# Rows of a graph layer scattered in groups of four, each group tied to TensorE's progress in the next block

## The chip, the core and the metric

The kernel runs on one core of one Trainium2 chip. The metric is device time in microseconds (us) of one execution; the time of a kernel is the median of several. Times inside an execution are read from a hardware trace of one profiled execution.

## The reference, cut to what matters

There are 6,250 nodes with 64 features, 206,250 directed edges (each drawn edge in both directions and one loop per node, sorted by destination before the call) with 64 features each. Per edge a first layer with 128 hidden values is computed; the hidden values are summed per target node and counted. What follows is small and per node.

```python
msg = concat([x[col], edge_attr], axis=1)          # per edge, 128 values
h = relu(msg @ W1a.T + b1a)                        # per edge, 128 hidden values
h = h @ W1b.T + b1b
sums = segment_sum(h, row, num_segments=n_nodes)   # summed per node
agg = sums / maximum(counts, 1)[:, None]
z = relu(concat([x, agg]) @ W2a.T + b2a) @ W2b.T + b2b
x = layernorm(x + concat([z, x]) @ Wr.T + br)
```

The kernel sums `relu(...)` per node, and applies `W1b` after the sum.

## The kernel before, in words

**Blocks.** The edges are cut into 124 blocks (`NGR`) of 13 tiles (`BLK`) of 128 edges. Edges of a block belong to scattered nodes, so they are sorted on the chip: the kernel computes the hidden values of a block's edges, counts with one-hot matmuls which slot of a table in DRAM each edge gets (slots are grouped by bins of 128 nodes), and GpSimd (POOL in the profile) scatters the rows there with indirect DMAs. A row is 130 numbers: 128 hidden values, a one for the count, and the node's place in its bin. Some blocks later the SyncE queue reads whole bins back in tiles of 128 rows (`read`, L1454), VectorE makes one-hot matrices of them (`nodes_of`, L1483) and TensorE sums a bin with one matmul per tile (`summed`, L1502); VectorE adds the result to the node's total (`collect`, L1562).

**Two kinds of block.** In blocks 4 to 103 ("joined" here) a part of the tiles goes another way: groups of 3 tiles (`JOIN`) are sorted inside the block by matmuls with one-hot `marks` (`join`, L1264), copied by ScalarE to `rj` (L1269), taken through the first layer (`join_rows`, L1277, with the ReLU at L1280), and scattered four rows at a time as a "quad" (L1363). `joined(k)` is 2 (3 in every second block from 9 to 25), so such a block has 2 quads and 7 single rows (`direct(k)`; 3 quads and 4 rows with three groups). The other blocks, "direct" here, have 13 single rows. A "row" below is one indirect DMA of L1392: one tile of 128 edges, 128 x 130 numbers. There are 985 rows and 209 quads in all. A row's number `j` is its tile's number in the block: 6 to 12 with two groups, 9 to 12 with three, 0 to 12 in direct blocks.

**One pass of the main loop (block k) on TensorE,** in this order: the counts of block k+1 (L1091 to L1095); all but the last part of the block's first layer (`hidden`, L1352, its ReLU L1355 writes `orow`); the ranks of the groups of block k+1 (`join_ranks`, L1118 to L1130), which need `of_quads` (L1105) from VectorE, which needs the counts; the first half of a group of sums (`sum_first`); the last part of `hidden`; `join` for groups 0 and 1; `join_rows` for group 0, then 1 (a third group follows in the same way); the second half of the sums (`sum_rest`), and in the direct blocks further whole groups of sums (`sum_next`). Sums are dealt out by `RATES`: about 13 tiles per joined block, 9 with three groups, and up to 50 in direct blocks.

**What sets the order.** TensorE, ScalarE, VectorE and SyncE work in the written order (`manual_schedule`). GpSimd's order is the framework's: it sorts the scatters by when they can go by its own plan, so that rows with nothing to wait for move ahead of others. `scatter(k)` issues the quads and rows of a block. Four buffers of rows (`ROWS`) let several blocks stand open. Each DMA goes to one of eight semaphores in turn (DMASW0 to DMASW7 in listings) and waits for the DMA that had it before.

**The pace.** For blocks 9 to 117 (`PACED`, L474) some rows of block k also wait for a matmul of block k+1, by the table `pace`: with two groups row 6 for column 9 of `hidden` (the end of its first part), row 8 for column 12 (the end of its last part), row 10 for `join_rows` 0, row 12 for `join_rows` 1; in direct blocks row 0 for column 9, row 2 for the first half of the sums, row 7 for column 12, row 11 for the rest of the sums. The rows between have no such wait. Blocks 118 to 123 have none at all.

## Time and profile before

| | |
|---|---|
| median of 3 runs | 2108.51 us (2105.86 to 2118.02) |
| profiled execution | 2113.43 us, span in the trace 2111.6 us |
| TensorE | busy 1648.5 us, 78% of the span, 10901 matmuls |
| VectorE | busy 1376.4 us, 65% |
| GpSimd | busy 1153.6 us, 55% |
| ScalarE | busy 1105.0 us, 52% |
| mean DMA rate | 188 GB/s |

A page of the profile gives busy times per engine, the span in 40 slices, the chain of work that ended last, and the costliest groups of instructions (line, engine, operation, output and input, count, busy time, mean, and the idle time just ahead of them with what ended most of it). A table of windows gives the busy time of each engine in a stretch of the trace, with TensorE's granted clock as a share of full speed (PEclk), the mean busy share of the DMA engines and GB/s. A timeline lists instructions with start, length and, in brackets, the idle time of that engine before them and what ended it; "remote" and "issue" mean that no instruction on the core was found that ended it just then.

### The profile page before, as it was taken

To read this page: it belongs to the slowest core of one execution; us is meant where nothing else is said; L and a number is where in the kernel's file an instruction comes from. 1 tells how busy PE (TensorE), PEld (TensorE's weight loads), DVE (VectorE), ACT (ScalarE), POOL (GpSimd) and SP (SyncE) were. 2 spreads that over 40 slices of the span, in tenths; PEclk is the share of its full clock that TensorE was granted. 3 is DMA by queue.
4 is the path that set the end of the run, shared out by engine and by line. 5 is a ranking of instruction groups with operands and counts; after the bars stand their busy time and mean duration, and the time that the engine had idled before them with its cause. 6 is when DMAs were issued, how large, how long until landed. Compare 5 with 4: busy or idle time off the path is not lost.

```text
span 2111.6 us, 33441 instructions
## 1 busy us (share of the span) xinstructions
PE 1648.5 (78%) x10901; PEld 1455.0 (69%) x10901; DVE 1376.4 (65%) x3210; ACT 1105.0 (52%) x2246; POOL 1153.6 (55%) x1268
## 2 busy tenths in 40 slices
PE   5577877768887888788778887877867778677787
PEld 4466766657776777677667776776767667566676
DVE  5377777656667777677776777776755555454377
ACT  2257777666666566566666666656622223222007
POOL 6464655565555566566665665655655545544400
PEclk7578988889999899999998999989978878777899
DMA  6556667665656567566556555555668667565472
GB/s 163 162 171 220 234 224 243 214 211 176 209 183 204 169 201 211 169 195 188 181 174 182 175 173 163 186 157 170 168 201 277 200 190 208 170 183 172 147 216 66
DMA packets 243142, 396.32 MB, mean 188 GB/s; under 512 B 43621, under 2 KB 177895, under 8 KB 242703
## 3 DMA queue, kind: packets, MB, share of 16 engines
q1 hardware_dynamic: 162109, 225.24, 37.7%
q0 software_dynamic: 48240, 121.28, 16.4%
q10 hardware_dynamic: 32610, 47.58, 6.5%
q8 instruction: 89, 1.46, 0.3%
q14 instruction: 94, 0.77, 0.1%
HBM read 218.49 MB, written 175.44 MB: 187 GB/s over the span
## 4 chain that ended last, share of the span: by engine, by line
PE 57%; issue 11%; DVE 10%; ACT 10%; another core or an unknown queue 8%; DMA 3%; POOL 1%; SPq 0%; ACTq 0%; DVEq 0%; POOLq 0%
PE h_ps L1502 22%; PE h_ps L1264 10%; PE h_ps L1352 9%; PE h_ps L1277 7%; DVE oh L1483 2%; DVE marks L1232 2%; ACT rhs L1317 2%; ACT rj L1269 1%; ACT orow L1355 1%; DMA rows<-orow,rowidx 1%; DMA rt<-rows 1%; ACT orow L1280 1%; ACT marks L1237 1%; PE cnt_ps L1091 1%
## 5 line engine op out<-in xcount | busy, mean ns | idle before, releaser
L1392 POOL DMA_INDIRECT rows<-orow,rowidx x985 | 947.2, 962 | 769.4 <-issue 207.4
L1502 PE MATMUL h_ps<-rt,oh 128*128 128x129 f32 x4056 | 602.3, 303 | 126.4 <-issue 105.4
L1502 PEld LDWEIGHTS h_ps<-rt,oh 128*128 128x128 f32 x4056 | 554.3, 215 | 151.9 <-issue 135.7
L1355 ACT ACTIVATE orow<-h_ps 128x384 f32<-128x384 f32 (+1 forms) x287 | 153.3, 537 | 657.5 <-PE h_ps L1352 360.7
L1277 PE MATMUL h_ps<-mv,rj 128*128 128x130 f32 x1672 | 256.1, 305 | 136.3 <-ACT rj L1269 73.5
L1264 PE MATMUL h_ps<-marks,side 128*128 128x512 f32 x1254 | 343.7, 423 | 23.8 <-ACT xr_now L1652 10.6
L1277 PEld LDWEIGHTS h_ps<-mv,rj 128*128 128x128 f32 x1672 | 232.6, 210 | 174.4 <-ACT rj L1269 89.1
L1562 DVE TENSOR_TENSOR part<-part,h_ps 128x387 f32<-128x387 f32 (+2 forms) x249 | 122.6, 493 | 312.5 <-remote 147.7
L1483 DVE TENSOR_TENSOR oh<-ramp,rt 128x768 f32<-128x768 bf16 (+3 forms) x440 | 321.3, 765 | 7.2 <-DMA rt<-rows 7.0
L1352 PE MATMUL h_ps<-mv,rhs 124*128 124x128 f32 x1970 | 297.3, 298 | 16.8 <-issue 9.2
L1264 PEld LDWEIGHTS h_ps<-marks,side 128*128 128x128 f32 x1254 | 245.1, 204 | 79.5 <-issue 11.6
L1352 PEld LDWEIGHTS h_ps<-mv,rhs 124*128 124x128 f32 x1970 | 267.1, 209 | 20.4 <-issue 10.6
L1232 DVE TENSOR_TENSOR marks<-quad_ramp,ramp 128x1024 fp32r<-128x1024 f32 x209 | 250.9, 1204 | 0.0
L1363 POOL DMA_INDIRECT quads<-orow,qidx x209 | 200.4, 959 | 88.8 <-ACT orow L1280 39.1
L1280 ACT ACTIVATE orow<-h_ps 128x260 f32<-128x260 f32 x418 | 142.6, 388 | 90.8 <-PE h_ps L1277 28.0
L1105 DVE TENSOR_SCALAR of_quads<-cnt_ps 128x98 bf16<-128x98 f32 x100 | 26.6, 266 | 247.0 <-remote 84.2
L1269 ACT COPY rj<-h_ps 128x512 f32<-128x512 f32 x209 | 118.8, 588 | 120.8 <-PE h_ps L1264 67.6
L1238 ACT ACTIVATE marks<-marks,ones 128x512 fp32r<-128x512 f32 x209 | 151.0, 722 | 6.8
L1237 ACT ACTIVATE marks<-quad_ramp,z_act 128x512 fp32r<-128x512 f32 x209 | 149.5, 715 | 0.0
L1049 DVE TENSOR_TENSOR_SCAN had<-ramp,bins 128x400 bf16<-128x400 bf16 (+1 forms) x124 | 135.0, 1089 | 14.9 <-ACT bins L1070 1.2
L1315 ACT ACTIVATE rhs<-rhs,from_win 60x896 f32<-60x896 bf16 (+1 forms) x116 | 130.4, 1124 | 2.8
L1317 ACT ACTIVATE rhs<-rhs,ones 60x896 f32<-60x896 f32 (+1 forms) x116 | 130.2, 1123 | 2.9
(189 smaller groups left out, 1535.6 us busy)
## 6 DMA issues: line engine op xcount, KB each, us to landing
rt<-rows SPq DMA_DIRECT2D x138, 390.0 KB
rt<-quads SPq DMA_DIRECT2D x98, 390.0 KB
rhs<-in_edgeT SPq DMA_DIRECT2D x91, 224.0 KB
rt<-rows SPq DMA_DIRECT2D x103, 195.0 KB
enat<-in_edgeJ SPq DMA_DIRECT2D x91, 192.0 KB
rows<-orow,rowidx POOLq DMA_INDIRECT x985
rows<-padrow ACTq DMA_DIRECT2D x12, 1300.0 KB
quads<-padrow ACTq DMA_DIRECT2D x11, 1300.0 KB
```

Source lines behind the costliest of these rows:

```text
L1232: nc.vector.tensor_tensor(m[:, :n, :], all_q[:, None, :].to_broadcast([P, n, QUAD * P]), z[:, :n, None].to_broadcast([P, n, QUAD * P]), op ...
L1237: nc.scalar.activation(m[:, t, :], all_q, AF.Square, bias=z_acts[k][:, i * JOIN + t : i * JOIN + t + 1], scale=-1.0)
L1264: nc.tensor.matmul(ps, s[:, p, i * JOIN + t, :], m[:, t, :], start=t + p == 0, stop=t == JOIN - 1 and p == 1,)
L1277: done[k, f"join{i}"] = nc.tensor.matmul(ps[:, j, :], rj[:, (g0 + j) * P : (g0 + j + 1) * P], m, start=True, stop=True).ins.name
L1280: nc.scalar.activation(mrow[:, g0 : g0 + 2, :], ps, AF.Relu)
L1317: nc.scalar.activation(rhs[D:WIDE, :], rhs[D:WIDE, :], AF.Relu, bias=ones[D:WIDE, :1], scale=-1.0)
L1352: done[k, c] = nc.tensor.matmul(ps[:, j, :], rhs[:WIDE, of * P : (of + 1) * P], m[:WIDE, :H], start=True, stop=True).ins.name
L1355: nc.scalar.activation(orow_of(k, k0, n)[:, :, :H], ps[:, :n, :], AF.Relu)
L1363: s = nc.gpsimd.indirect_dma_start(out=qep.rows.rearrange("(q r) f -> q (r f)", r=QUAD), out_offset=bass.IndirectOffsetOnAxis(ap=qidx[:, q ...
L1392: s = nc.gpsimd.indirect_dma_start(out=ep_.rows, out_offset=bass.IndirectOffsetOnAxis(ap=rowidx[:, k % RING * BLK + j : k % RING * BLK + j ...
L1483: nc.vector.tensor_tensor(res[:, at_tile : at_tile + nb * n, :], ramp[:, None, :].to_broadcast([P, nb * n, P]), node[:, :, None].to_broadc ...
L1502: m = nc.tensor.matmul(of_bin(b), oh[:, at_tile, :], rt[:, j * n + t, : H + 1], start=t0 + t == st.lo[b], stop=t0 + t == st.hi[b] - 1,)
```

## The change

The table `pace` goes. Each piece of TensorE's work on a block is now written down as it is issued (`phase`): its size in matmul columns times passes, and its last matmul. `reached(k + 1, share)` gives the last matmul of block k+1 up to which at most that share of the block's written work is done; for a share of 0 that is the last one of block k itself. Every row of blocks 9 to 117 now waits for one of these. The share steps up after every fourth row, where the quads count as rows ahead: with two groups rows 6 and 7 have share 0, rows 8 to 11 have 4/9, row 12 has 8/9; with three groups row 9 has 0 and rows 10 to 12 have 4/7; in direct blocks rows 0 to 3 have 0, rows 4 to 7 have 4/13, rows 8 to 11 have 8/13 and row 12 has 12/13.

For a block with two groups and one group of 12 tiles of sums, the work is 20080 in all: 2048 `hidden`, 4128 first half of sums, 1536 `hidden` (7712 so far), two times 3072 `join`, two times 2080 `join_rows` (each written down in halves of 1040), 2064 rest of the sums. 4/9 of that is 8924, so rows 8 to 11 wait for the end of `hidden` in block k+1; 8/9 is 17849, so row 12 waits for the first half of the second `join_rows` (16976). A direct block has 6656 of `hidden` and, with 48 tiles, 24768 of sums; 4/13 of 31424 is 9669, so rows 4 to 7 wait for the first half of the first sums (9248).

```diff
@@ join
+            phase(k, 2 * JOIN * QUAD * P, name)
@@ join_rows
+                phase(k, 4 * W * 2, name)
@@
-        done = {}
+        phases = [[] for _ in range(NGR + 1)]
+        def phase(k, work, name):
+            phases[k].append(((phases[k][-1][0] if phases[k] else 0) + work, name))
+        def reached(k, share):
+            names = [name for at, name in phases[k] if at <= share * phases[k][-1][0]]
+            return names[-1] if names else phases[k - 1][-1][1]
@@ hidden
+                phase(k, 4 * H * n, name)
@@ scatter
-            pace = (
-                {9: BLK - 1, 10: "join0", 11: "join1", 12: "join2"} if j0 == 3 * JOIN
-                else {6: 9, 8: BLK - 1, 10: "join0", 12: "join1"} if j0 == 2 * JOIN
-                else {j0: 9, j0 + 2: "first", 7: BLK - 1, 9: "join0", 11: "rest"}
-            )
-                later = (min(k + 1, NGR - 1), pace.get(j))
-                if k in PACED and later in done:
+                later = reached(k + 1, (j - j0 + joined(k)) // 4 * 4 / (BLK - j0 + joined(k))) if k in PACED else None
+                if later:
-                        s.ins, done[later],
+                        s.ins, later,
@@ sum_first, and sum_rest in the same way
+            phase(k, *summed(g.st, g.reads, g.oh, lambda b: g.ps[:, b - g.b0, :], g.half))
```

The order of TensorE, ScalarE, VectorE and SyncE stays as it is; GpSimd's changes. Two places show it. In the rows below L1363 is a quad and L1392 a row of before, L1377 and L1401 the same of the change; `orow0` to `orow3` are the four buffers (block k uses buffer k mod 4), and the brackets hold what an instruction waits for.

GpSimd in the joined part before, from row 6 of block 61 (`orow1`), among rows of block 60 (`orow0`) and block 62 (`orow2`):

```order
L1392 DMA rows0_64<-orow1_142,rowidx_105 125440x130 [waits DMASW0_49,DVE_49,Activation_49]
L1392 DMA rows0_64<-orow1_142,rowidx_105 125440x130 [waits DMASW1_49]
L1392 DMA rows0_64<-orow0_141,rowidx_105 125440x130 [waits DMASW2_49,PE_49]
L1392 DMA rows0_64<-orow1_142,rowidx_105 125440x130 [waits DMASW3_49,Activation_49]
L1392 DMA rows0_64<-orow0_141,rowidx_105 125440x130 [waits DMASW4_49,PE_49]
L1363 DMA quads_67<-orow1_142,qidx_224 54976x520 [waits DMASW5_49,DVE_49,Activation_49]
L1392 DMA rows0_64<-orow0_141,rowidx_105 125440x130 [waits DMASW6_49,PE_49]
L1363 DMA quads_67<-orow1_142,qidx_224 54976x520 [waits DMASW7_49,Activation_49]
L1392 DMA rows0_64<-orow1_142,rowidx_105 125440x130 [waits DMASW0_49,PE_49]
L1392 DMA rows0_64<-orow2_143,rowidx_105 125440x130 [waits DMASW1_49,DVE_49,Activation_49]
L1392 DMA rows0_64<-orow2_143,rowidx_105 125440x130 [waits DMASW2_49]
L1392 DMA rows0_64<-orow1_142,rowidx_105 125440x130 [waits DMASW3_49,PE_49]
```

The same place after the change, from the first quad of block 61 to the second quad of block 62:

```order
L1377 DMA quads_67<-orow1_142,qidx_224 54976x520 [waits DMASW2_49,DVE_49,Activation_49]
L1377 DMA quads_67<-orow1_142,qidx_224 54976x520 [waits DMASW3_49,Activation_49]
L1401 DMA rows0_64<-orow0_141,rowidx_105 125440x130 [waits DMASW4_49,PE_49]
L1401 DMA rows0_64<-orow1_142,rowidx_105 125440x130 [waits DMASW5_49,PE_49]
L1401 DMA rows0_64<-orow1_142,rowidx_105 125440x130 [waits DMASW6_49]
L1401 DMA rows0_64<-orow1_142,rowidx_105 125440x130 [waits DMASW7_49,PE_49]
L1401 DMA rows0_64<-orow1_142,rowidx_105 125440x130 [waits DMASW0_49]
L1401 DMA rows0_64<-orow1_142,rowidx_105 125440x130 [waits DMASW1_49]
L1401 DMA rows0_64<-orow1_142,rowidx_105 125440x130 [waits DMASW2_49]
L1401 DMA rows0_64<-orow1_142,rowidx_105 125440x130 [waits DMASW3_49,PE_49]
L1377 DMA quads_67<-orow2_143,qidx_224 54976x520 [waits DMASW4_49,DVE_49,Activation_49]
L1377 DMA quads_67<-orow2_143,qidx_224 54976x520 [waits DMASW5_49,Activation_49]
```

Before, the rows of two blocks alternate, and rows of a block without a wait for TensorE go ahead of its quads; now a block's rows follow its quads, with a wait for TensorE at rows 6, 8 and 12.

GpSimd in the direct part before, from the first row to go of block 107 (`orow3`), among rows of block 106 (`orow2`):

```order
L1392 DMA rows0_64<-orow3_144,rowidx_105 125440x130 [waits DMASW1_49,DVE_49,Activation_49]
L1392 DMA rows0_64<-orow3_144,rowidx_105 125440x130 [waits DMASW2_49]
L1392 DMA rows0_64<-orow2_143,rowidx_105 125440x130 [waits DMASW3_49,PE_49]
L1392 DMA rows0_64<-orow3_144,rowidx_105 125440x130 [waits DMASW4_49,Activation_49]
L1392 DMA rows0_64<-orow3_144,rowidx_105 125440x130 [waits DMASW5_49]
L1392 DMA rows0_64<-orow3_144,rowidx_105 125440x130 [waits DMASW6_49]
L1392 DMA rows0_64<-orow2_143,rowidx_105 125440x130 [waits DMASW7_49,PE_49]
L1392 DMA rows0_64<-orow3_144,rowidx_105 125440x130 [waits DMASW0_49,Activation_49]
L1392 DMA rows0_64<-orow3_144,rowidx_105 125440x130 [waits DMASW1_49]
L1392 DMA rows0_64<-orow3_144,rowidx_105 125440x130 [waits DMASW2_49,Activation_49]
L1392 DMA rows0_64<-orow3_144,rowidx_105 125440x130 [waits DMASW3_49]
L1392 DMA rows0_64<-orow2_143,rowidx_105 125440x130 [waits DMASW4_49,PE_49]
```

The same place after the change, rows 0 to 11 of block 107:

```order
L1401 DMA rows0_64<-orow3_144,rowidx_105 125440x130 [waits DVE_49,DMASW5_49,PE_49,Activation_49]
L1401 DMA rows0_64<-orow3_144,rowidx_105 125440x130 [waits DMASW6_49]
L1401 DMA rows0_64<-orow3_144,rowidx_105 125440x130 [waits DMASW7_49]
L1401 DMA rows0_64<-orow3_144,rowidx_105 125440x130 [waits DMASW0_49]
L1401 DMA rows0_64<-orow3_144,rowidx_105 125440x130 [waits DMASW1_49,PE_49,Activation_49]
L1401 DMA rows0_64<-orow3_144,rowidx_105 125440x130 [waits DMASW2_49]
L1401 DMA rows0_64<-orow3_144,rowidx_105 125440x130 [waits DMASW3_49]
L1401 DMA rows0_64<-orow3_144,rowidx_105 125440x130 [waits DMASW4_49,Activation_49]
L1401 DMA rows0_64<-orow3_144,rowidx_105 125440x130 [waits DMASW5_49,PE_49]
L1401 DMA rows0_64<-orow3_144,rowidx_105 125440x130 [waits DMASW6_49]
L1401 DMA rows0_64<-orow3_144,rowidx_105 125440x130 [waits DMASW7_49]
L1401 DMA rows0_64<-orow3_144,rowidx_105 125440x130 [waits DMASW0_49,Activation_49]
```

Before, nine rows of a block go without a wait for TensorE, mixed with four of the block before that have one; now one block's rows follow each other, and the first of every four waits for TensorE.

More of the change, by code (lines that the diff above doesn't have):

```diff
@@ L1263, in join @@
                 for p in range(2):
-                    nc.tensor.matmul(
+                    name = nc.tensor.matmul(
                         ps, s[:, p, i * JOIN + t, :], m[:, t, :],
                         start=t + p == 0, stop=t == JOIN - 1 and p == 1,
-                    )
+                    ).ins.name
+            phase(k, 2 * JOIN * QUAD * P, name)
             rj = turned[k, i] = top.rjs[(join_at[k] + i) % 2]
@@ L1276, in join_rows @@
                 for j in range(2):
-                    done[k, f"join{i}"] = nc.tensor.matmul(
+                    name = nc.tensor.matmul(
                         ps[:, j, :], rj[:, (g0 + j) * P : (g0 + j + 1) * P], m, start=True, stop=True
                     ).ins.name
+                phase(k, 4 * W * 2, name)
                 nc.scalar.activation(mrow[:, g0 : g0 + 2, :], ps, AF.Relu)
@@ L1351, in hidden @@
                     of = c - (BLK - direct(k))
-                    done[k, c] = nc.tensor.matmul(
+                    name = nc.tensor.matmul(
                         ps[:, j, :], rhs[:WIDE, of * P : (of + 1) * P], m[:WIDE, :H], start=True, stop=True
                     ).ins.name
+                phase(k, 4 * H * n, name)
                 nc.scalar.activation(orow_of(k, k0, n)[:, :, :H], ps[:, :n, :], AF.Relu)
@@ L1384, in scatter @@
                         tc.declare_no_dep(s.ins, group=f"qreads{j}", reason="later edges have later slots")
-            pace = (
-                {9: BLK - 1, 10: "join0", 11: "join1", 12: "join2"} if j0 == 3 * JOIN
-                else {6: 9, 8: BLK - 1, 10: "join0", 12: "join1"} if j0 == 2 * JOIN
-                else {j0: 9, j0 + 2: "first", 7: BLK - 1, 9: "join0", 11: "rest"}
-            )
             for j in range(j0, BLK):
@@ L1492, in summed @@
         def summed(st, reads, oh, of_bin, bins=None):
-            at_tile = 0
+            at_tile, work = 0, 0
             for b0, nb, t0, n, rt in reads:
@@ L1506, in summed @@
                         at_tile += 1
-            return m.ins.name
+                        work += 4 * (H + 1)
+            return work, m.ins.name
         def reads_of(st):
@@ L1570, in sum_first @@
             g.half = range(g.b0, g.b0 + -(-g.nb // 2))
-            done[k, "first"] = summed(g.st, g.reads, g.oh, lambda b: g.ps[:, b - g.b0, :], g.half)
+            phase(k, *summed(g.st, g.reads, g.oh, lambda b: g.ps[:, b - g.b0, :], g.half))
             return g
@@ L1575, in sum_rest @@
             if g.nb > len(g.half):
-                done[k, "rest"] = summed(
+                phase(k, *summed(
                     g.st, g.reads, g.oh, lambda b: g.ps[:, b - g.b0, :], range(g.half.stop, g.b0 + g.nb)
-                )
+                ))
             totals.append(g)
```

## The prediction

> **What bounds the kernel now.** I read the page first, then the stages by windows, then the order of events inside one block.
>
> ```profile
> PE 1648.5 (78%) x10901; PEld 1455.0 (69%) x10901; DVE 1376.4 (65%) x3210; ACT 1105.0 (52%) x2246; POOL 1153.6 (55%) x1268
> PE 57%; issue 11%; DVE 10%; ACT 10%; another core or an unknown queue 8%; DMA 3%; POOL 1%; SPq 0%; ACTq 0%; DVEq 0%; POOLq 0%
> L1392 POOL DMA_INDIRECT rows<-orow,rowidx x985 | 947.2, 962 | 769.4 <-issue 207.4
> L1502 PE MATMUL h_ps<-rt,oh 128*128 128x129 f32 x4056 | 602.3, 303 | 126.4 <-issue 105.4
> ```
>
> TensorE is on most of the chain that ended last and yet idle for 22% of the span, and 105.4 us of the idle time ahead of the sums is "issue": at those matmuls nothing in the trace says what they waited for. The stages differ:
>
> ```profile
> 360.00:1510.00 1150.00, 938.92 (x6388) 824.24 (x6388) 820.42 (x1992) 737.43 (x1464) 682.62 (x711) 0.92 0.60 185
> 1615.00:1820.00 205.00, 158.21 (x1077) 146.11 (x1077) 107.04 (x181) 54.84 (x75) 112.09 (x118) 0.83 0.68 202
> 1820.00:2016.00 196.00, 140.40 (x893) 127.41 (x893) 83.49 (x136) 33.00 (x47) 97.60 (x102) 0.75 0.53 160
> ```
>
> The first is the joined part (711 scatters, nine to a block, so 79 blocks of 14.56 us), the second the paced direct blocks (118 scatters, 13 to a block: 9.1 blocks of 22.6 us), the third mostly the unpaced ones. TensorE idles 211 us in the first, 2.67 us a block, and 46.8 us in the second, 5.15 us a block.
>
> What it idles for shows inside a block. These rows are from the joined part; between the first and the last GpSimd row here lie four more scatters, each 0.30 us behind the one before.
>
> ```profile
> 1004.35 0.96 POOL L1392 DMA_INDIRECT rows<-orow,rowidx  x1 [1.45 <-PE h_ps L1264]
> ...
> 1008.78 1.12 PE L1352 MATMUL h_ps<-mv,rhs 124*128 124x128 f32 x8
> ...
> 1010.66 0.96 POOL L1363 DMA_INDIRECT quads<-orow,qidx  x1 [0.30 <-issue]
> 1013.02 0.26 DVE L1105 TENSOR_SCALAR of_quads<-cnt_ps 128x98 bf16<-128x98 f32 x1 [5.72 <-remote]
> 1013.11 0.60 ACT L1355 ACTIVATE orow<-h_ps 128x512 f32<-128x512 f32 x1 [3.12 <-remote]
> 1013.34 0.29 PE L1118 MATMUL cnt_ps<-joh,before_w 128*128 128x300 bf16 x1 [3.44 <-DVE of_quads L1105]
> 1013.36 0.96 POOL L1392 DMA_INDIRECT rows<-orow,rowidx  x1 [1.73 <-DVE of_quads L1105]
> ```
>
> TensorE ended the eight `hidden` matmuls at 1009.90. Their ReLU on ScalarE began at 1013.11, and VectorE's `of_quads`, whose counts are older still, at 1013.02: both when GpSimd had come to a scatter that had to wait, 2.4 us after the last scatter of the run began. So I read it this way: **while scatters follow each other without a pause, word from one engine to another comes late, and it comes when the run ends.** The mechanism inside the chip is not in the trace; the size can be read by the length of the run. Each window below goes from the first scatter of a run to the first of the next; the last number in the POOL column is the scatters, give or take one at an edge.
>
> ```profile
> 1013.36:1018.27 4.91, 4.82 (x28) 4.60 (x28) 4.77 (x11) 3.47 (x7) 2.87 (x4) 0.65 0.61 227
> 1018.27:1021.97 3.70, 3.70 (x24) 3.25 (x22) 3.56 (x13) 1.94 (x4) 1.91 (x2) 1.00 0.50 130
> 1021.97:1032.49 10.52, 8.44 (x63) 7.18 (x62) 7.20 (x17) 7.29 (x16) 6.71 (x8) 1.00 0.59 187
> 1032.49:1041.70 9.21, 6.69 (x53) 6.06 (x54) 4.18 (x10) 5.54 (x13) 5.74 (x7) 1.00 0.65 188
> 1091.67:1097.82 6.15, 5.00 (x40) 4.50 (x40) 4.07 (x9) 2.89 (x8) 3.83 (x4) 0.88 0.71 230
> 1097.82:1105.55 7.73, 5.49 (x35) 4.46 (x33) 7.45 (x20) 4.60 (x9) 5.01 (x5) 1.00 0.40 126
> 1623.46:1629.54 6.08, 5.74 (x51) 5.38 (x49) 5.94 (x9) 1.33 (x3) 3.83 (x4) 1.00 0.89 281
> 1675.64:1691.80 16.16, 10.53 (x75) 9.45 (x75) 4.74 (x10) 4.88 (x7) 10.54 (x11) 0.85 0.53 152
> 1749.48:1765.76 16.28, 11.30 (x81) 10.89 (x81) 5.86 (x12) 5.07 (x7) 10.54 (x12) 0.78 0.56 173
> ```
>
> TensorE's idle time, stretch less busy: joined runs of 3, 2, 7, 6, 4, 5 scatters cost 0.09, 0, 2.08, 2.52, 1.15, 2.24 us; direct runs of 4, 11, 11 cost 0.34, 5.63, 4.98 us. The first four rows together are two blocks (18 scatters, 28.3 us) and 4.69 us of idle.
>
> **The change, part by part.** It adds no instruction and moves nothing on TensorE, ScalarE, VectorE or SyncE. It sets where GpSimd's runs are broken. GpSimd's own time for a scatter in a run, 0.96 + 0.30 = 1.26 us, stays, and so does the data moved.
>
> *Direct blocks, rows of blocks 104 to 117 (14 blocks).* Now a block is a run of 11 and some single rows:
>
> ```profile
> 1723.16 0.96 POOL L1392 DMA_INDIRECT rows<-orow,rowidx  x1 [1.58 <-ACT orow L1355]
> ...
> 1735.78 0.95 POOL L1392 DMA_INDIRECT rows<-orow,rowidx  x1 [0.30 <-issue]
> 1745.80 0.96 POOL L1392 DMA_INDIRECT rows<-orow,rowidx  x1 [9.07 <-PE h_ps L1502]
> ```
>
> After 12.6 us of scatters GpSimd waits 9.07 us for a sum on TensorE that the run itself had held up. With the change the rows go 4, 4, 4, 1, each group behind a matmul at 0, 29%, about 60% and about 90% of the next block. Seen from TensorE: three groups of four cost between 0.34 us (the direct row) and 1.15 us (the joined row) each, 1.0 to 3.5 us in place of 5.15, a gain of 1.7 to 4.1 us a block. Seen from GpSimd: 13 x 1.26 = 16.4 us, and each of four waits adds to its 0.30 us pause. A wait that ends a run took 1.73, 1.58 and 1.45 us of idle in the rows above, 1.15 to 1.43 more than a pause; the least that I can bound it by is nothing, where the signal is there. Four of them between 0.7 (half) and 1.43 us give a floor of 19.2 to 22.1 us against 22.6. I take 1.0 us a wait, 20.4 us, a gain of 2.2 us a block, since GpSimd's floor is the tighter of the two: **14 x 2.2 = 31 us**, with bounds of 7 (22.1) and 48 us (19.2). Blocks 118 to 123 aren't paced before or after: nothing.
>
> A run also costs clock behind it:
>
> ```profile
> 1729.20:1739.00 9.80, 4.08 (x16) 2.30 (x14) 0.04 (x1) 0.00 (x0) 5.74 (x6) 0.79 0.33 101
> 1740.40:1745.80 5.40, 5.40 (x28) 5.40 (x29) 4.15 (x8) 0.00 (x0) 0.00 (x0) 0.57 0.85 295
> ```
>
> TensorE is busy for 4.08 of 9.80 us, and then runs without a gap at 0.57 of its clock. If full clock came back, those 5.40 us would take 3.1, 2.3 us a block more; since GpSimd is the floor above, I count nothing for it, and keep 14 x 2.3 = 32 us as what the forecast could be short by. The Trainium skill ("TensorE: Matmul & The Clock Gate", section "What's actually happening") says that the clock halves after one idle window of about 3.4 us and comes back after one busy window; the 0.57 behind the long stall agrees. By that rule groups of four, idle for 1 us at a time, would never drop the clock, and the direct blocks would gain the 2.3 us as well.
>
> *Joined blocks with two groups (79 in the window).* Now rows of two blocks alternate and make runs of 2 to 7. By the order of GpSimd after the change a block's nine scatters stand: quad 0, quad 1, row 12 of the block before, rows 6 and 7, then rows 8 to 11. Quad 0 can go at 79% of the block's TensorE work, quad 1 and row 12 at 85 to 90%, rows 6 and 7 at its end, rows 8 to 11 at 38% of the next. In time, with 14.56 us: 11.5, 13.1, 14.6 and 20.1 us. Four scatters from 13.1 end at 18.1, before 20.1; the next four end at 25.1, before the next quad 0 at 26.1. So I expect runs of 1, 4 and 4. By the rows above that is 0 + 1.15 + 1.15 = 2.30 us idle a block, against 2.35 in the two quoted blocks and 2.67 over the stage: a gain of 0.05 to 0.37. I take 0.1, close to the lower because the first run of four lies on the handover of the counts (L1105), which is where the waits are dearest now:
>
> ```profile
> PE h_ps L1277 <- ACT rj L1269: 60.8, 31, 3.9
> PE cnt_ps L1118 <- DVE of_quads L1105: 47.4, 35, 4.8
> ```
>
> The second run, from 38% to 73% of the block, lies on `join` and `rj`; that wait doesn't go either. **79 x 0.1 = 8 us.** Bounds: runs of 4, 3 and 2 (1.15 + 0.09 + 0 = 1.24 us) would gain 1.43 us a block, 113 us; runs of 5 and 4 (3.39 us) would lose 0.72 a block, 57 us. Blocks 9 to 26, half of them with seven scatters only, leave GpSimd more slack, and I count nothing there; at the joined rates their 18 blocks would be 2 us either way of 0.1.
>
> *The wait added to every row.* Behind a waiting row on GpSimd stand only further scatters and quads; who waits for those are the reads some blocks later, and the eight DMA semaphores. Rows go later than before by up to most of a block. The reads are issued two to three blocks behind, so I count nothing; if a read came to wait, the sums would wait for it, and a block with no sums ready would lose up to its 3.9 us of sums (13 x 303 ns).
>
> *The sum.* 31 + 8 = 39 us off the profiled execution's 2113.4: 2074. That execution is 4.9 us above the median of 2108.5, so the time to compare is **2070 us**.
>
> **The rivals.**
>
> *GpSimd becomes the bound in the joined part (slower).* Nine scatters are 11.34 us of 14.56. The quoted two blocks have four waits that end a run, two a block; the new order has waits at quad 0, quad 1, row 12, row 6 and row 8, of which I count three as real. At 1.0 us each three waits make 14.3 us, just under today's block, and four make 15.3, 0.8 over: 79 x 0.8 = 63 us lost, 7 to 31 gained in the direct blocks, 2140 to 2165. It decides from four real waits a block on, or three at over 1.07 us. For it: GpSimd waits 1.45 us and more at the quoted ends of runs. Against it: much of that wait is today TensorE's being late. The Trainium skill ("Perfetto Trace Analysis", section "What 'DMA-bound' means") puts a solid track of DMA slices on the issuing engine down to descriptor generation and advises larger descriptors; by that rule breaking up runs gains nothing where GpSimd is solid. The 9.07 us pause above speaks against it for the direct blocks; nothing quoted excludes it for the joined ones. Chance 0.28.
>
> *The change doesn't do what it says.* Where GpSimd comes to a wait whose matmul is long done, it goes on, and groups flow together into runs as long as before. The joined part then stays, and the direct part keeps a third to a half of its gain: 2095 to 2110. Chance 0.17.
>
> *More than forecast.* Runs of 4, 3 and 2 in the joined part for half of the blocks (57 us) with 48 us in the direct part, or the clock as well: 1980 to 2030. Chance 0.12.
>
> **How the numbers follow.** The forecast has 0.43, and spans 2045 (direct 48, joined 0.2 a block) to 2097 (direct 7, joined nothing). The range has to reach into the slower rival and the better one: 2015 to 2150 leaves out about 2 in 10. About 0.5% (10.5 us) is what a measurement of this kernel can tell from no change. Faster by more: the forecast, the better rival, and none of the second, 0.54; within it: 0.18, the second rival and a little of the others; slower: 0.28.
>
> **What would show it.** In the windows of the paced direct blocks, 118 scatters in about 185 us rather than 205, GpSimd's rows in fours, no idle of 9 us on it, and a granted clock above 0.83. In the joined part runs of 1, 4 and 4, and idle of TensorE near 2.5 us a block; `PE cnt_ps` waiting for `of_quads` no less than now. I am wrong if the idle of GpSimd ahead of L1401 for TensorE grows in the joined stage while the block grows with it (first rival), if runs of eight or more remain (second), or if short runs idle TensorE as much as long ones, which would fell the reading itself.

## The result and the profile after

The change takes **2201.78 us** (median of 4 runs, 2178.41 to 2231.31) against 2108.5. The ratio leaves out the longest of the four as a slow run: 1.0392, 95% interval 1.0338 to 1.0447. Slower by 3.9%, where 2070 us was forecast. The profiled execution took 2178.41 us, the shortest of the four, with a span of 2176.6, 65.0 more than the span before. So the two traces account for 65 us, and not for the whole difference of the medians (93 us).

The same work in the same three stretches: 76 joined blocks (26 to 101 on TensorE), then the last two joined blocks and the direct blocks with a pace, then the tail from the first run of 13 scatters that has no wait for TensorE. Windows of before:

```profile
400.00:1502.00 1102.00, 898.35 (x6150) 789.78 (x6150) 786.06 (x1902) 705.02 (x1400) 656.26 (x685) 0.93 0.60 184
1502.00:1892.00 390.00, 288.64 (x1923) 267.02 (x1921) 204.48 (x344) 107.01 (x154) 209.36 (x219) 0.81 0.67 202
1892.00:2111.60 219.60, 173.53 (x1188) 154.60 (x1187) 130.34 (x308) 59.38 (x213) 62.23 (x65) 0.85 0.53 153
```

Windows of the change:

```profile
413.00:1603.00 1190.00, 925.80 (x6162) 822.74 (x6160) 782.75 (x1902) 710.06 (x1404) 655.09 (x683) 0.90 0.56 171
1603.00:1958.00 355.00, 266.65 (x1919) 247.98 (x1918) 204.17 (x344) 106.04 (x154) 212.55 (x222) 0.87 0.74 222
1958.00:2176.60 218.60, 171.54 (x1188) 153.47 (x1186) 130.28 (x308) 59.23 (x212) 62.23 (x65) 0.87 0.54 154
```

The joined blocks lost 88 us (1190 against 1102 for 76 blocks, 1.16 us a block), the blocks before them 13 (413 against 400), the direct blocks **gained 35** (355 against 390), the tail is the same. Of the 88 us, 61 are idle time of TensorE (264 us against 204) and 27 are longer busy time at a lower granted clock (0.90 against 0.93; busy time times clock is 833 and 836 us). Of the 35 us, 13 are idle time (88 against 101) and 22 busy time, with the clock at 0.87 in place of 0.81. The groups of instructions, here of the whole execution, say where TensorE waits; of before:

```profile
L1277 PE MATMUL h_ps<-mv,rj 128*128 128x130 f32 x1672 | 256.1, 305 | 136.3 <-ACT rj L1269 73.5 <-issue 36.8 <-ACT orow L1280 21.1
L1118 PE MATMUL cnt_ps<-joh,before_w 128*128 128x300 bf16 x100 | 32.1, 321 | 100.5 <-DVE of_quads L1105 70.6 <-issue 28.4 <-DVE marks L1232 1.5
```

and of the change (L1278 is the old L1277):

```profile
L1278 PE MATMUL h_ps<-mv,rj 128*128 128x130 f32 x1672 | 232.3, 286 | 75.2 <-ACT orow L1282 33.7 <-ACT rj L1270 27.0 <-ACT rhs L1319 6.8
L1118 PE MATMUL cnt_ps<-joh,before_w 128*128 128x300 bf16 x100 | 32.9, 329 | 261.5 <-issue 155.6 <-DVE of_quads L1105 98.4 <-DVE marks L1232 7.5
```

Idle ahead of `join_rows` fell by 61 us, idle ahead of the ranks of the groups (L1118), which need VectorE's `of_quads`, rose by 161. The timeline of the change shows one block, with most rows left out. L1365 is `hidden`, L1264 `join`, L1270 its copy to `rj`, L1278 `join_rows`, L1282 its ReLU, L1095 the counts. The GpSimd rows left out are rows 9 and 10, with gaps of 0.30 us.

```profile
1022.00 0.90 PE L1365 MATMUL h_ps<-mv,rhs 124*128 124x128 f32 x6
1022.65 2.98 PE L1264 MATMUL h_ps<-marks,side 128*128 128x512 f32 x12
1024.31 0.59 ACT L1270 COPY rj<-h_ps 128x512 f32<-128x512 f32 x1 [0.89 <-PE h_ps L1264]
1024.56 0.95 POOL L1401 DMA_INDIRECT rows<-orow,rowidx  x1 [4.22 <-DVE hit_q L1160]
1025.47 1.55 PE L1278 MATMUL h_ps<-mv,rj 128*128 128x130 f32 x12
1027.34 0.94 ACT L1282 ACTIVATE orow<-h_ps 128x260 f32<-128x260 f32 x3
1028.33 0.95 POOL L1401 DMA_INDIRECT rows<-orow,rowidx  x1 [0.30 <-issue]
1028.53 0.39 ACT L1282 ACTIVATE orow<-h_ps 128x260 f32<-128x260 f32 x1 [0.24 <-issue]
1029.59 0.96 POOL L1377 DMA_INDIRECT quads<-orow,qidx  x1 [0.30 <-issue]
1030.86 0.96 POOL L1377 DMA_INDIRECT quads<-orow,qidx  x1 [0.30 <-issue]
1031.35 0.30 PE L1095 MATMUL cnt_ps<-joh,one_w 128*128 128x100 bf16 x3
1032.12 0.96 POOL L1401 DMA_INDIRECT rows<-orow,rowidx  x1 [0.31 <-issue]
1034.78 0.26 DVE L1105 TENSOR_SCALAR of_quads<-cnt_ps 128x98 bf16<-128x98 f32 x1 [2.81 <-remote]
1034.95 0.95 POOL L1401 DMA_INDIRECT rows<-orow,rowidx  x1 [1.87 <-remote]
1035.09 0.29 PE L1118 MATMUL cnt_ps<-joh,before_w 128*128 128x300 bf16 x1 [2.49 <-issue]
1036.21 0.97 POOL L1401 DMA_INDIRECT rows<-orow,rowidx  x1 [0.30 <-issue]
1040.01 0.96 POOL L1401 DMA_INDIRECT rows<-orow,rowidx  x1 [2.83 <-PE h_ps L1365]
```

Rows 8 to 11 go at 1024.56 to 1028.33, and the quads and row 12 follow without a pause: a run of seven whose last scatter begins at 1032.12. The counts were done at 1031.65; `of_quads` begins at 1034.78. Then rows 6 and 7 make a run of two, and GpSimd stands idle for 2.83 us until `hidden` is at its end. The windows of two rounds, each a run of seven and a run of two:

```profile
1007.86:1018.12 10.26, 7.15 (x47) 6.12 (x46) 5.24 (x15) 6.12 (x14) 6.71 (x8) 0.97 0.44 119
1018.12:1024.56 6.44, 6.28 (x34) 5.71 (x34) 6.16 (x18) 4.13 (x8) 1.91 (x3) 0.74 0.61 196
1024.56:1034.95 10.39, 7.29 (x58) 6.60 (x57) 5.26 (x11) 5.10 (x12) 6.69 (x7) 1.00 0.61 186
1034.95:1040.01 5.06, 4.89 (x28) 4.66 (x28) 4.89 (x12) 3.62 (x7) 1.93 (x2) 0.66 0.22 79
```

A run of seven leaves TensorE idle for 3.1 us, a run of two for 0.17: 3.27 us a block, where the two blocks of before in the prediction had 2.35. The whole stretch goes the same way. Cut at every gap of GpSimd above 0.6 us, its 76 blocks have 184 runs before and 151 after. Runs of seven went from 14 to 47. TensorE's idle time in them, counted from the start of a run to the start of the next, went from 31.5 to 164.4 us. Runs of two cost it 0.3 us each before and 0.2 after.

### The profile page after: what moved, and what is told of

It reads as the page before. It is cut to its first block, busy times and chain, and to the rows that moved or that the text cites. A ratio compares the mean times of both kernels' runs of the same rounds, so it can differ in the third digit from the quotient of the medians.

```text
span 2176.6 us, 33416 instructions
## 1 busy us (share of the span) xinstructions
PE 1648.5 (76%) x10901; PEld 1465.6 (67%) x10901; DVE 1372.7 (63%) x3210; ACT 1108.4 (51%) x2246; POOL 1152.9 (53%) x1268
## 4 chain that ended last, share of the span: by engine, by line
PE 41%; issue 17%; DVE 16%; another core or an unknown queue 11%; ACT 6%; POOL 6%; DMA 3%; DVEq 0%; SPq 0%; ACTq 0%; POOLq 0%
PE h_ps L1511 17%; PE h_ps L1365 7%; PE h_ps L1264 7%; POOL rows L1401 4%; PE h_ps L1278 3%; DVE marks L1232 3%; DVE oh L1492 2%; POOL quads L1377 1%; ACT rhs L1319 1%; DMA rows<-orow,rowidx 1%; DMA rt<-rows 1%; DVE part L1572 1%; DVE hit_q L1160 1%; PE h_ps L878 1%
## 5 line engine op out<-in xcount | busy, mean ns | idle before, releaser
L1401 POOL DMA_INDIRECT rows<-orow,rowidx x985 | 946.5, 961 | 835.8 <-issue 249.0
L1264 PE MATMUL h_ps<-marks,side 128*128 128x512 f32 x1254 | 340.1, 422 | 3.0 <-ACT xr_now L1662 1.6
L1365 PE MATMUL h_ps<-mv,rhs 124*128 124x128 f32 x1970 | 313.1, 306 | 32.7 <-issue 19.0
L1365 PEld LDWEIGHTS h_ps<-mv,rhs 124*128 124x128 f32 x1970 | 282.1, 218 | 39.0 <-issue 23.1
L1278 PE MATMUL h_ps<-mv,rj 128*128 128x130 f32 x1672 | 232.3, 286 | 75.2 <-ACT orow L1282 33.7
L1278 PEld LDWEIGHTS h_ps<-mv,rj 128*128 128x128 f32 x1672 | 213.3, 192 | 105.3 <-ACT orow L1282 42.4
L1264 PEld LDWEIGHTS h_ps<-marks,side 128*128 128x128 f32 x1254 | 247.2, 205 | 54.6 <-issue 2.3
L1377 POOL DMA_INDIRECT quads<-orow,qidx x209 | 200.5, 959 | 86.6 <-issue 55.5
L1118 PE MATMUL cnt_ps<-joh,before_w 128*128 128x300 bf16 x100 | 32.9, 329 | 261.5 <-issue 155.6
L1120 PEld LDWEIGHTS <-one_w 128*128 128x128 bf16 x200 | 20.8, 104 | 281.4 <-issue 276.2
L1282 ACT ACTIVATE orow<-h_ps 128x260 f32<-128x260 f32 x418 | 140.4, 388 | 101.0 <-PE cnt_ps L1095 31.1
L1270 ACT COPY rj<-h_ps 128x512 f32<-128x512 f32 x209 | 120.4, 587 | 136.4 <-PE h_ps L1264 107.0
```

The lines of the kernel that those rows point to most:

```text
L1264: name = nc.tensor.matmul(ps, s[:, p, i * JOIN + t, :], m[:, t, :], start=t + p == 0, stop=t == JOIN - 1 and p == 1,).ins.name
L1278: name = nc.tensor.matmul(ps[:, j, :], rj[:, (g0 + j) * P : (g0 + j + 1) * P], m, start=True, stop=True).ins.name
L1365: name = nc.tensor.matmul(ps[:, j, :], rhs[:WIDE, of * P : (of + 1) * P], m[:WIDE, :H], start=True, stop=True).ins.name
L1377: s = nc.gpsimd.indirect_dma_start(out=qep.rows.rearrange("(q r) f -> q (r f)", r=QUAD), out_offset=bass.IndirectOffsetOnAxis(ap=qidx[:, q ...
L1401: s = nc.gpsimd.indirect_dma_start(out=ep_.rows, out_offset=bass.IndirectOffsetOnAxis(ap=rowidx[:, k % RING * BLK + j : k % RING * BLK + j ...
```

## The experiments

**Two kinds of chip.** The kernel before took 1608 to 1611 us (medians) on six of the chips that the runs went to, and 2077 to 2106 us on three others; the recorded 2108.5 is of the second kind. They are called short and long chips below. Two of the short ones were used twice and were short both times; whether the chip itself makes the difference isn't shown by more than that. Each ratio is with before on the same chip.

**The change in halves, and two of its waits moved.** e1 keeps the table of before for the joined blocks and has shares in the direct ones, e2 the reverse; e4 and e5 edit the change (the lines of e1 and e2 that bring the table back are left out):

```diff
@@ e1 (e2 with the two sides exchanged)
+later = (done.get((k + 1, pace.get(j))) if joined(k) else reached(k + 1, ...)) if k in PACED else None
@@ e4: scatter, behind each quad
+tc.add_manual_dep(s.ins, phases[k][-1][1], ...)
@@ e5
-later = reached(k + 1, (j - j0 + joined(k)) // 4 * 4 / (BLK - j0 + joined(k)))
+later = reached(k + 1, {0: 0, 1: 2 if joined(k) == 2 else 4, 2: 8, 3: 12}[(j - j0 + joined(k)) // 4] / (BLK - j0 + joined(k)))
```

> Joined blocks keep the pace table of before, direct blocks 104 to 117 wait by shares as in the change. In the trace of the change the stretch of the direct blocks was 35 us shorter and the joined part 101 us longer than before. Theory A (the loss is all in the joined part, the direct part gains): 2073 us, range 2060 to 2090. Rival (the two stretches depend on each other: the direct blocks gained because the joined part ran late): 2100 to 2120.

> The other half alone: joined blocks wait by shares, direct blocks keep the pace table. Theory A: 2202 + 35 = 2237 us, range 2200 to 2260. Rival (the stretches depend on each other): about as the change, 2180 to 2205.

> The change, and every quad of blocks 9 to 117 waits in addition for the last matmul of its own block. One wait more on GpSimd, none less. Theory A (a long run of scatters that lies over the handover of the counts costs the time; quads that flow on behind rows 8 to 11 make a run of seven there): the run breaks before the quads, runs become 5 and 4, the handover of the counts falls into the first two us of a run; block 13.3 to 14.3 us instead of 15.65, total 2010 to 2090. Theory B (each wait makes GpSimd drain, and GpSimd sets the block's time): one more wait a block, 15.65 + 0.5 to 1.0 us, total 2230 to 2290.

> The change, but rows 8 to 11 of blocks with two groups wait for the first part of hidden of the next block (share 2/9) instead of its last part (4/9). Same number of waits. Theory A: rows 6 to 11 become one run of six that begins at the block's end, the quads and row 12 a run of three before it; the handover of the counts is at the start of a run; block 13.8 to 14.8 us, total 2060 to 2130. Theory B (number of waits sets the time): 2180 to 2205, as the change; or down by what row 8 waits less.

Measured on a short chip (before 1608.62): 1610.11, 1613.02, 1613.11 and 1614.07 us, ratios 1.0013 (0.9999 to 1.0028), 1.0028 (1.0015 to 1.0040), 1.0028 (1.0014 to 1.0041) and 1.0023 (1.0008 to 1.0039). None of the expectations, all made for a long chip, was tested. Then the change itself:

> The change itself, unaltered. The four kernels run so far on a chip where the kernel before takes 1608.6 us, not 2108.5, came out within 0.3% of it, although in the recorded comparison one half of the change was worth plus 101 us and the other minus 35. Theory A2 (on that chip word between engines is not held up by scatters, GpSimd's own 1.26 us per scatter sets the time, and the waits of the change lie under it): if the kernel before takes 1608 us again, 1605 to 1620; if it takes 2108 us, 2180 to 2230. Rival (the change loses 3 to 4% whatever the chip does): 1660 to 1680 beside 1608, or 2180 to 2230 beside 2108.

Measured: 1611.59 us beside 1607.77, ratio 1.0025 (1.0012 to 1.0038): theory A2, and its rival falls. On a short chip the loss of 3.9% isn't there. What differs shows in the joined part of e1 (L1410 is a row there):

```profile
800.89 0.96 POOL L1410 DMA_INDIRECT rows<-orow,rowidx  x1 [0.30 <-issue]
802.15 0.95 POOL L1410 DMA_INDIRECT rows<-orow,rowidx  x1 [0.30 <-DMA quads<-orow,qidx]
802.65 0.30 PE L1095 MATMUL cnt_ps<-joh,one_w 128*128 128x100 bf16 x3
802.99 0.26 DVE L1105 TENSOR_SCALAR of_quads<-cnt_ps 128x98 bf16<-128x98 f32 x1 [0.52 <-PE cnt_ps L1095]
803.41 0.96 POOL L1410 DMA_INDIRECT rows<-orow,rowidx  x1 [0.30 <-ACT marks L1237]
803.75 0.30 PE L1118 MATMUL cnt_ps<-joh,before_w 128*128 128x300 bf16 x1
```

Here the scatters have no pause, and `of_quads` begins 0.04 us after the counts' end at 802.95, in the middle of a run. The groups and a window of the change on a short chip (f1):

```profile
L1118 PE MATMUL cnt_ps<-joh,before_w 128*128 128x300 bf16 x100 | 30.2, 302 | 13.7 <-DVE of_quads L1105 13.6
307.00:1174.00 867.00, 807.04 (x6152) 730.97 (x6151) 779.51 (x1902) 705.26 (x1400) 651.19 (x674) 1.00 0.76 233
```

13.7 us of idle at L1118 against 261.5 with the same kernel, and 867 us for the 76 blocks: 11.41 us a block, beside 9 x 1.26 = 11.34 us of GpSimd. On a short chip GpSimd's scatters nearly fill a block, and no such hold-up shows.

**No pace at all, and one scatter more.** g1 takes every wait for TensorE away (`PACED = range(0)`); g3 is before with a 14th scatter in each of blocks 27 to 103, which writes row 12 into a table that nothing reads.

> No row waits for TensorE's work on the next block at all, in any block: the pace of both kernels is taken out. Theory A2 (on chips where the kernel before takes 1608 us word between engines isn't held up by scatters, and GpSimd sets the time at 1.26 us a scatter): within 0.5% of before, 1603 to 1616 us. Theory B (waits on GpSimd cost time by themselves, which would then explain the recorded loss of the change): faster than before by 1% or more, below 1593 us. If the chip holds word up (before at 2108 us): A says slower than before, 2120 to 2250.

> The kernel before, and in each of blocks 27 to 103 the scatter of row 12 once more into a spare table that nothing reads: 77 scatters more. If GpSimd's 1.26 us a scatter sets the time of these blocks: 77 x 1.26 = 97 us more, 1690 to 1715 us. If it doesn't (TensorE or VectorE set it): 0 to 40 us more. If the chip holds word up (before at 2108 us): 50 to 150 us more.

Both went to a long chip (before 2106.3). g1: 2308.26 us, ratio 1.0954 (1.0887 to 1.1022). That waits on GpSimd cost the time by themselves (theory B) falls, since without any the kernel is 9.5% slower. A's range (2120 to 2250) was left upwards. g3 (two runs): 2225.44, ratio 1.0565 (1.0505 to 1.0626), 119 us for 77 scatters, 1.55 us each. That is within the 50 to 150 us expected and more than GpSimd's own 1.26 us; that the rest comes from longer runs is argued, not shown. The joined blocks of g1 took 1241 us with TensorE idle for 282, 3.7 us a block. Runs of seven, 57 of them, hold 187 us of that, 3.3 us each:

```profile
423.00:1664.00 1241.00, 958.64 (x6155) 846.31 (x6154) 784.13 (x1902) 710.30 (x1401) 662.22 (x686) 0.87 0.54 164
```

e1 and e4 were sent again and once more went to a short chip:

> The kernel of e1_direct_new once more (joined blocks by the table of before, direct blocks by shares), in the hope of a chip on which the kernel before takes 2108 us. There: theory A, 2073 us, range 2060 to 2090; the rival (the stretches depend on each other) 2100 to 2120. On a chip where before takes 1608 us: 1605 to 1616.

> The kernel of e4_quads_at_end once more (the change, and every quad waits for the end of its own block's TensorE work), on such a chip. Theory A (a run of seven scatters over the handover of the counts costs the time): runs of 5 and 4, block 13.3 to 14.3 us, total 2010 to 2090. Theory B (waits cost time by themselves), already in trouble since taking out all waits cost 9.5%: 2230 to 2290. On a chip where before takes 1608 us: 1608 to 1618.

1611.98 and 1612.5 us beside 1608.17 (1.0019 and 1.0024, intervals 1.0005 to 1.0033 and 1.0013 to 1.0035).

**Four ways in one kernel.** Since a run says something only on a long chip, m1, m2 and m3 hold the ways side by side, 19 joined blocks each (20 in the last), in different orders, and pace blocks 118 to 122 by shares too (the order here is m2's):

```diff
+WAYS = [(0, 'table'), (27, 'early'), (46, 'end'), (65, 'shares'), (84, 'table'), (104, 'shares')]
+if way_of(k) == "end":
+    tc.add_manual_dep(s.ins, phases[k][-1][1], ...)
+if way_of(k) == "table":
+    later = done.get((k + 1, pace.get(j)))
+else:
+    n = (j - j0 + joined(k)) // 4 * 4
+    if way_of(k) == "early" and n == 4:
+        n = 2
+    later = reached(k + 1, n / (BLK - j0 + joined(k)))
```

> Four ways of waiting in one kernel, 19 joined blocks each: blocks 27 to 45 by the table of before, 46 to 64 by shares as in the change, 65 to 83 by shares and every quad behind its own block's end, 84 to 103 by shares with rows 8 to 11 behind the first part of hidden; the direct blocks 104 to 122 by shares (118 to 122 had no wait before). On a chip where before takes 2108 us, theory A: 14.5, 15.65, 13.3 to 14.3 and 13.8 to 14.8 us a block, in this order; direct blocks 104 to 117 35 us less than before, 118 to 122 10 to 20 us less; total 2050 to 2080. Theory B (waits cost time by themselves): the third stretch the slowest, over 15.65. On a chip where before takes 1608 us: 11.4 us a block in all four, 1605 to 1618.

> As m1_four_ways with the stretches in another order: blocks 27 to 45 rows 8 to 11 early, 46 to 64 quads behind their block's end, 65 to 83 by shares as in the change, 84 to 103 by the table. On a chip where before takes 2108 us, theory A: 13.8 to 14.8, 13.3 to 14.3, 15.65 and 14.5 us a block; direct blocks 104 to 117 35 us less than before, 118 to 122 10 to 20 us less; total 2050 to 2080. Theory B: the second stretch the slowest, over 15.65. On a chip where before takes 1608 us: 11.4 us a block in all four, 1605 to 1618.

> The four ways with the stretches in a third order: blocks 27 to 45 by shares as in the change, 46 to 64 by the table, 65 to 83 shares with rows 8 to 11 early, 84 to 103 shares with the quads behind their block's end; direct blocks 104 to 122 by shares. On a chip where before takes 2070 to 2110 us, by what the same places took in before, the change and m2_four_ways: 16.4, 14.7, about 14.8 and about 14.9 us a block; total 2080 to 2100. If the differences came from the place and not from the way: 16.0, 14.9, 14.6 and 14.8, as in m2_four_ways. Where before takes 1608 us: 11.4 in all, 1608 to 1618.

m1 and m3 went to short chips (1612.54 beside 1610.59, 1610.08 beside 1608.43, one run each). m2 went to a long one: 2094.01 beside 2099.96, one run each, where theory A had 2050 to 2080. Its stretches of 19 blocks, in order early, end, shares, table:

```profile
406.80:710.50 303.70, 229.67 (x1495) 199.51 (x1493) 185.42 (x460) 183.10 (x369) 162.34 (x170) 0.88 0.58 180
710.50:994.00 283.50, 232.94 (x1598) 203.15 (x1597) 200.86 (x488) 174.51 (x349) 161.97 (x170) 0.93 0.61 187
994.00:1271.60 277.60, 218.81 (x1526) 193.78 (x1524) 198.44 (x477) 171.69 (x337) 164.61 (x172) 0.94 0.58 175
1271.60:1553.60 282.00, 227.18 (x1542) 202.15 (x1541) 200.07 (x478) 175.39 (x346) 168.00 (x175) 0.92 0.55 167
```

The first three places in the change, all by shares:

```profile
413.30:724.90 311.60, 238.31 (x1495) 210.62 (x1493) 183.88 (x460) 183.91 (x370) 162.70 (x170) 0.86 0.56 175
724.90:1031.30 306.40, 239.99 (x1599) 215.05 (x1597) 201.11 (x488) 177.65 (x351) 164.67 (x172) 0.90 0.57 174
1031.30:1316.20 284.90, 222.58 (x1526) 198.36 (x1524) 197.88 (x477) 172.41 (x337) 163.40 (x171) 0.93 0.56 170
```

And the second place in before:

```profile
677.00:956.10 279.10, 232.47 (x1600) 204.69 (x1598) 203.28 (x489) 176.88 (x351) 165.86 (x173) 0.93 0.62 192
```

With one wait more the second stretch takes 283.5 us in place of 306.4, 14.9 a block for 16.1, and TensorE idles 50.6 us instead of 66.4. The third stretch goes by shares in both kernels and is the yardstick: 277.6 us in m2, 284.9 in the change. So some 7 of the 23 us may come from the chip or the place, and some 16 are left for the wait, of the 27 us that the change had lost to before there. By this one run the quads that flow on behind rows 8 to 11 are a good part of the loss. Most runs are of 5 or 4 (15 and 17 of 39), as expected. GpSimd in two of its blocks, where L1421 is a row and L1386 a quad, and the scatters left out have gaps of 0.30 us:

```profile
816.70 0.96 POOL L1421 DMA_INDIRECT rows<-orow,rowidx  x1 [1.27 <-PE h_ps L1539]
...
821.76 0.96 POOL L1421 DMA_INDIRECT rows<-orow,rowidx  x1 [0.30 <-issue]
824.42 0.96 POOL L1421 DMA_INDIRECT rows<-orow,rowidx  x1 [1.70 <-PE h_ps L1264]
...
829.47 0.96 POOL L1421 DMA_INDIRECT rows<-orow,rowidx  x1 [0.30 <-issue]
832.33 0.96 POOL L1386 DMA_INDIRECT quads<-orow,qidx  x1 [1.90 <-ACT orow L1359]
```

In the first of these runs, from 816.70, the counts end at 817.54 and `of_quads` begins at 818.07, while the second scatter is under way: so early in a run word isn't late. But 14.9 us isn't the 13.3 to 14.3 of theory A, and not less than before had there (279.1 us, 14.7). Runs of 5 still leave TensorE idle for 1.97 us each, 29.5 of the 50.6 us, and runs of 4 for 0.38. Rows 8 to 11 early (first stretch, 16.0 a block; the change had 16.4) missed its 13.8 to 14.8: its waits show `join_rows` waiting for `rj` up to 8.6 us, since rows 6 to 11 flow on into longer runs. Seven runs of 8 to 10 hold 42.6 of its 73.6 us of idle time. Runs of 5 cost 0.52 us there and runs of 4 2.13, so the length alone doesn't set the price.

```profile
PE h_ps L1278 <- ACT rj L1270: 34.7, 9, 8.6
```

The third stretch, with the change's own way, took 14.6 us a block where 15.65 was expected; the change had 15.0 at that place and 16.1 to 16.4 in the two before. The last, by the table, took 14.8 where 14.5 was expected. Against before in the four places (277.3, 279.1, 267.7 and 278.4 us) the change lost 34, 27, 17 and 8 us. So the loss per block depends on the place as well as on the way, and m3, which was to tell them apart, went to a short chip. That stays open.

**Table for the joined blocks, shares for the direct ones to 122.** This is e1 with `PACED = range(PRE, 123)`, sent three times:

> Joined blocks by the table of before, direct blocks 104 to 122 by shares (118 to 122 had no wait before). In the trace of m2_four_ways the stretch from block 103 to the end took 539 us with this pace, against 609 in the profiled run of before. On a chip where before takes 2105 us, theory A: 2105 - 70 = 2035 us, range 2020 to 2060. Rival (the stretches depend on each other, the joined part gives the gain back): 2080 or more. On a chip where before takes 1608 us: 1605 to 1616.

> The kernel of e6_direct_to_122 once more, since that ran on a chip where before takes 1608 us. On a chip where before takes 2105 us, theory A: 2035 us, range 2020 to 2060. Rival (the joined part gives the gain of the direct part back): 2080 or more. Where before takes 1608 us: 1608 to 1616.

> The kernel of e6_direct_to_122 a third time, on another chip. On a chip where before takes 2105 us, theory A: 2035 us, range 2020 to 2060. Rival (the joined part gives the gain of the direct part back): 2080 or more. Where before takes 1608 us: 1608 to 1616.

On short chips 1611.84 and 1611.94 us (1.0014, 1.0004 to 1.0024, and 1.0018, 1.0006 to 1.0031). On a long chip **2036.65 us** beside 2076.98, ratio 0.9789 (0.9727 to 0.9852): faster than before by 40 us. Against before at 2105 us, theory A had 70 us (45 at least) and the rival, in which the joined part gives the gain back, 25 at most. The 40 us lie between, so a part may be given back. Theory A's 70 us came from the stretch behind the 76 joined blocks, in m2 538.6 us against 609.4. Here are its windows of before and of k2:

```profile
1502.20:2111.60 609.40, 461.96 (x3108) 421.52 (x3105) 334.61 (x651) 166.18 (x366) 271.39 (x284) 0.82 0.62 184
1500.40:2035.50 535.10, 421.92 (x3107) 389.10 (x3105) 335.00 (x651) 165.37 (x366) 272.82 (x284) 0.90 0.71 210
```

That stretch is 74 us shorter, but the trace of before is of an execution of 2113 us, and beside k2 before takes 2077. How much of the 74 us is the chip can't be told without a trace of before there. The halves in whole kernels went to a short chip again:

> Joined blocks by the table of before, direct blocks 104 to 117 by shares. On a chip where before takes 2070 to 2110 us: 25 to 40 us less than before on that chip (theory A); within 10 us of it (the joined part gives it back). Where before takes 1608 us: 1608 to 1616.

> Joined blocks by shares, direct blocks by the table. On a chip where before takes 2070 to 2110 us: 80 to 140 us more than before on that chip (theory A). Where before takes 1608 us: 1608 to 1616.

> The change, and every quad behind its own block's end. In m2_four_ways 19 blocks took 14.9 us each this way where the change took 16.1 at the same place. On a chip where before takes 2070 to 2110 us: 60 to 90 us less than the change would there, and 10 to 40 us less than before (theory A); more than the change (waits cost time by themselves). Where before takes 1608 us: 1608 to 1618.

1612.02, 1612.72 and 1613.36 us beside 1609.19 (1.0017, 1.0007 to 1.0026; 1.0025, 1.0014 to 1.0036; 1.0027, 1.0016 to 1.0038). So the plus of the joined half and the minus of the direct half are read from the stretches of two traces; each as a whole kernel on a long chip wasn't measured.

## Why the prediction was wrong, step by step

- **The bound** (scatters in an unbroken run hold up word between engines, and word comes when the run ends): the trace after shows the same for runs of seven, and g1 bears it out on a long chip. "When the run ends" is too strict: early in a run of m2's second stretch word came in 0.53 us. On short chips the hold-up isn't seen. What in the chip does it wasn't found.
- **The direct blocks, 31 us gained:** the size is right, the picture behind it only in part. 390 us became 355. GpSimd's pace is as forecast: in the trace after, four blocks in a row begin 20.1 us apart (1764.29 to 1844.67), where 20.4 was put. But the rows don't go in fours throughout. Of 200 scatters from 1638 to 1958 us, 81 go in runs of 4 and 5 and 108 in runs of 8 to 12. Those four blocks have two or three waits of 1.2 to 2.2 us each, not four of 1.3 (1.0 above the pause); that the sums agree is luck. TensorE's idle time fell by 13 us only, and not to the 1.0 to 3.5 us a block that were read from its side. 22 us of the gain are busy time at a higher clock, for which nothing had been counted.
- **The joined blocks, 8 us gained:** this is the step that failed, and its sign with it. It read "I expect runs of 1, 4 and 4". It turned shares of written work into times, and took one block's shares for all.
  - *The times.* From the end of `hidden` to the end of `join_rows` the written work is 10304 of 20080, which of 14.56 us makes 7.5. Measured, it took 5.6 us in the block shown above (1022.90 to 1028.49) and 4.6 us in the next (1039.73 to 1044.31). The two `join` took 2.98 us, not 6144/20080 of 14.56 = 4.5.
  - *The shares.* The block worked out ahead of the prediction (12 tiles of sums, 4128 in their first half) isn't among blocks 27 to 103. By the sizes that the kernel writes down, 37 of these 77 have 9 tiles of sums and 28 have 18, mostly in turn. With 9 tiles the work is 18532 and 4/9 of it 8236; `hidden` ends at 6680 and the first `join` at 9752 (in all but one of them), so rows 8 to 11 of the block before wait for `hidden`. With 18 tiles the work is 23176 and 4/9 of it 10300, so they wait for the first `join`. In all, 35 of the 77 blocks make them wait for that.
  - *What came of it.* Quad 0 was placed 6.0 us behind the go for rows 8 to 11 (26.1 against 20.1 us), with row 12 behind it. The block shown above has 18 tiles. There the first `join` is done by 1024.31, and rows 8 to 11 go from 1024.56, 1.66 us behind the end of `hidden`. Three of the four ReLUs of `join_rows`, the two of quad 0 among them, are over at 1028.28, 3.7 us behind the first of four scatters that need 5.04; the last is over at 1028.92. So the quads were ready when their turn came. The next block has 9 tiles. There rows 8 to 11 go from 1040.01, 0.28 us behind `hidden`; row 12 stands behind them there. Its matmul was done by 1044.31, it went without a pause at 1045.10, and the quads behind it at 1046.36 and 1047.62. Either way the run became 7. Its end lies on the handover of the counts: 3.1 us of idle time here and 3.5 on average over 47 runs, where 1.15 had been put.
- **Blocks 9 to 26, nothing:** 13 us lost in the stretch ahead of the 76 blocks.
- **The wait for `rj` "doesn't go either":** most of it did. Idle time ahead of `join_rows` fell from 136.3 to 75.2 us, the part put down to `rj` from 73.5 to 27.0; the handover of the counts took more than that back.
- **The rivals.** "GpSimd becomes the bound" gave 2140 to 2165 us, near the profiled 2178, but by another mechanism: its price was waits that drain GpSimd. The 76 blocks have fewer breaks after the change than before (151 against 184), g1 is 9.5% slower without any wait, and the second stretch of m2, with a wait more, is faster a block than the change. "Groups flow together into runs as long as before" is what happened, between the quads and the rows ahead of them; it was priced at no loss in the joined part, since the prediction didn't ask what the run would lie on.

## What to carry to other kernels

Place a wait by times from the trace, not by counted work: 7.5 us by counted columns took 4.6 to 5.6 us here, and a share of the work pointed at another matmul in every second block. Together that joined two groups into one. In this kernel a run of scatters cost by what lay under it as well as by its length, so ask for each group which one follows it and whether a pause is left. And measure a pacing on more than one chip, since what it cures may be there on some only.

## What was not expected of the hardware

The same program takes 1608 to 1611 us (medians) on some chips and 2077 to 2108.5 on others, with the same 1.26 us from scatter to scatter. On the first kind 27 scatters in a row leave TensorE busy for 33.57 of 36.30 us (the change, f1):

```profile
602.80:639.10 36.30, 33.57 (x256) 30.27 (x255) 31.90 (x77) 28.04 (x56) 25.95 (x27) 1.00 0.79 249
```

On the second a run of seven takes 3 us from it. The mean granted clock goes with it, 0.97 against 0.84 to 0.90: of the 323 us between the 76 blocks of the change on the two kinds (1190 against 867), 204 are TensorE's idle time and 119 longer busy time. The scatters' own transfers take no longer there: the packets of GpSimd's queue fill 16.4% of the span of the 16 DMA engines before (346 us of 2111.6) and 21.6% in f1 (347 us of 1608.1). Why the chips differ is open.
